# Moving the attention norm of six blocks into the stage before, through a DRAM tensor

## The chip, the cores and the metric

The kernel runs on one NeuronCore of a Trainium2 chip. It is written in Bass with the Tile layer, which places the tiles and sets the semaphores. The metric is the device time of one execution in microseconds; lower is better.

The engines are TensorE (PE, with its weight loads as PEld), VectorE (DVE), ScalarE (ACT), GpSimd (POOL) and SyncE (SP, used here to send DMAs).

## The reference

Four layers follow one another on x, 64 sequences of 64 tokens with 256 features, each with a condition vector of 64 values for each sequence:

```python
# layer 0: gated MLP with quantised activations and ternary weights
h = x * (scale * rsqrt(mean(x * x) + 1e-6))         # scale = cond @ norm_w.T + 1
val, gate = split(h @ up_w.T)
x = act_quant(val * gelu(gate)) @ weight_quant(down_w).T + x
# layer 1: attention, then SwiGLU
n = gamma * (x * rsqrt(mean(x * x) + 1e-6)) + beta  # gamma, beta from cond
x = x + alpha * attention(n)                        # 16 heads of 16 features
x = x + alpha2 * swiglu(gamma2 * rmsnorm(x) + beta2)
# layer 2: layernorm with a bias from cond; layer 3: an adapter whose weights
# are generated from cond for every sequence
```

The change concerns one term: `x * rsqrt(mean(x * x) + 1e-6)` ahead of the attention, called the attention norm here. It needs only the output of layer 0.

## The kernel before

The 4096 tokens are cut into 8 blocks of 512 tokens; a block is four tiles of 128 tokens. Three stages follow one another on the same engines. All operands of the products are float32, and a large product is made as three products of split halves (`mm3`, L87 to L89; `split` and `Splitter.turn` make the halves, the rounded one on ScalarE and the rest, by a subtraction, on VectorE or GpSimd).

**First stage** (`l0`). The loop runs over 32 tiles, n = 0 to 31, and two more steps. In step n TensorE makes the two halves of the up product (`upper(n, 0)` and `upper(n, 1)`, each with two PSUM banks); ScalarE makes the gelu (L454) and VectorE multiplies (`h`, L455). Then VectorE quantises (`quant(n)`, L461 to L466) and a DMA transposes the result (`qt`). Three steps later `lower(n - 3)` multiplies by the ternary weights (L480), and VectorE adds the input, which writes a quarter of the block's `x1` (L481). After the fourth tile of a block GpSimd sends `x1` to the DRAM tensor `x1d` (L483). In step n the output of tile n - 3 is written last, after `quant(n)`.

In between, the adapter's weights are generated: in the steps n = 5, 9, 12, 16, 19, 22, 25, 29 TensorE makes four groups of products (`gen_make`, L302, eight PSUM banks in all), ScalarE copies them out (`gen_stage`, L317), and GpSimd sends them to `s1d` and `s2d` (`gen_store`, L324). They stand between the two halves of the step. PSUM has eight banks, all shared in this stage. `hooks` is a table of more work by step: the steps 8 to 15 each split a piece of the attention weights (`splits.turn`, L221 on ScalarE and L222 on VectorE), and the steps from 25 on load and norm the first blocks of the attention and begin its products.

**Attention.** A loop over 16 units w, two to a block (`i, tp = divmod(w, 2)`). A unit computes the scores (`a_score`, L653), takes the maximum and the exponentials, transposes them on TensorE (`a_turn`, L694) with copies out of PSUM (`pts`, L696 on VectorE or L698 on ScalarE), and weighs the values of the unit before (`a_weigh`, L713, which reads `pts`). In between TensorE makes q, k and v of the next block (`a_ahead`, copied out as `qf`, `kb`, `vx`). The block after that is normed: `a_load` fetches `x1` (L588), `a_begin` squares it on ScalarE (`rms`, L236) and takes the root on GpSimd (`rsqrt`, L227 and L229), `a_scale` multiplies (`norm_tm`: L251 on ScalarE for block 2 and later, L253 on VectorE for the first two), and `norm_turn` transposes the result `xn` (L260) and applies gamma and beta (L263, L264); `split` makes `xh` and `xl` of it (L243, L244). The four PSUM banks of this stage go round in an explicit list, `pools["turn"]`, and `bank(tag, old)` says which entry from the front is taken.

**SwiGLU, layernorm and adapter** make the third stage.

The order of instructions on PE, ACT, DVE and POOL is the order in which the program issues them (`manual_schedule`). Each works strictly through its own list, so an instruction that waits holds back everything behind it. SP's DMAs are ordered by the Tile layer after the first few steps. Tiles of one tag share a fixed number of buffers: `x1` has five (`X1 = 5`, used by `xt`, `x1`, `ax1`, `ax2` and others), `xn` one, `rs`, `ss` and `st` two each. A tile that needs a buffer waits until the tile before it has been read for the last time, a store included.

Of the kernel before, what the change touches and what calls it, by code (L numbers as in the profile page):

```python
# [8 lines left out]
F32 = mybir.dt.float32  # L9
# [8 lines left out]
P = 128  # L18
NB = 64
L = 64  # L20
D = 256
# [15 lines left out]
def tile_kernel(ctx: ExitStack, tc, xT, x, condT, cw, upT, downT, qkvT, woT, ghT, outT_w,  # L37
# [6 lines left out]
    dram = ctx.enter_context(tc.tile_pool(name="dram", bufs=1, space=DRAM))  # L44
    x1d = dram.tile([NTOK, D], F32, name="x1d")
    x2d = dram.tile([NTOK, D], F32, name="x2d")
    alphad = dram.tile([3, NB, D], F32, name="alphad")
    s1d = dram.tile([2, NB, 128, BN], F32, name="s1d")
    s2d = dram.tile([2, NB, 64, D], F32, name="s2d")
# [274 lines left out]
                nc.gpsimd.dma_start(out=dst[:, :, c * GC:(c + 1) * GC], in_=stg[c * 64:(c + 1) * 64])  # L324


    def l0(hooks):
        pool = pools["a"]
        up = two(pool, "up", 2, 2 * FF)
# [141 lines left out]
        def lower(n):  # L471
            i, t = divmod(n, TT)
            am, qt = til.pop(n)
            if t == 0 and i > 0:
                blk[i][3] = block(f"x1_{i}")
            xt, x1 = blk[i][0], blk[i][3]
            nc.vector.tensor_scalar(am[:, 3:4], am[:, 1:2], wm, None, ALU.mult)
            py = bank("mm")
            for f in range(8):
                nc.tensor.matmul(py[:, :D], lhsT=qt[:, f, :], rhs=wq[:, f, :], start=f == 0, stop=f == 7)  # L480
            nc.vector.scalar_tensor_tensor(x1[:, t], py[:, :D], am[:, 3:4], xt[:, t], ALU.mult, ALU.add)  # L481
            if t == TT - 1:
                nc.gpsimd.dma_start(out=tok(x1d, i), in_=x1)  # L483
                del blk[i]

        def warm(n):

# [51 lines left out]
        for n in range(N + 2):  # L539
            if n < N:  # L540
                if n > 1:
                    upper(n, 0)
                if n == 0:
                    ternary_load()
                if n in visits:
                    for _ in range(4):
                        gen_make()
                        gen_stage()
                for _ in range(0 if n == 4 else 2 if n in visits and (n + 3 in visits or n == visits[-1]) else 1):
                    gen_load(ups[1][:, n % 2, n:n + 1] if n < 4 else None)  # L550
                    gen_store()
                upper(n, 1, "rest" if n < 2 else None)
                if n == 1:
                    ternary()
                    blk[0][3] = block("x1_0")
                if n == 4:
                    ternary_rest()
                if n % TT == 0 and n // TT + 1 < NBLK:
                    prep_load(n // TT + 1)
                if n % TT == 1 and n // TT + 1 < NBLK:  # L560
                    for _ in prep_parts(n // TT + 1):
                        pass
                if n % TT == 2 and n // TT + 1 < NBLK:
                    prep_scale(n // TT + 1)
            if n == N - 1:
                quant(n)
            for hook in hooks.get(n, ()):
                hook()

            if n < N - 1 and n != 5:  # L570
                quant(n)
            if n > 4:
                for k in range({5: 0, N + 1: N - 1}.get(n, n - 3), {N: N - 1, N + 1: N}.get(n, n - 2)):
                    lower(k)
            if n == 5:
                quant(n)


    ablk, units = {}, {}
# [6 lines left out]
    def a_load(i):  # L586
        x1 = block(f"ax1_{i}")
        nc.sync.dma_start(out=x1, in_=tok(x1d, i))  # L588
        ablk[i] = dict(x1=x1)

    def a_begin(i):
        ablk[i]["rs"] = rms(ablk[i]["x1"], f"a{i}")

    def a_scale(i):
        ablk[i]["n"] = norm_tm(ablk[i]["x1"], ablk[i]["rs"], f"a{i}", i > 1)

    def a_norm(i, c):
        norm_fm(*ablk[i]["n"], i, c, V_AG, V_AB)
# [42 lines left out]
    def a_score(w):  # L641

        i, tp = w // 2, w % 2
        pool = pools["b"]
        qf, kb = ablk[i]["qf"], ablk[i]["kb"]
        pS = banks("S", 4)
        for u in range(2):
            for m in range(2):
                for j in range(4):
                    js = slice(32 * j, 32 * (j + 1))  # L650
                    for h in range(2):
                        b = 4 * tp + 2 * u + h
                        nc.tensor.matmul(pS[h * 64:(h + 1) * 64, j, (2 * u + m) * P:(2 * u + m + 1) * P],  # L653
                                         lhsT=qf[js, m, b * L:(b + 1) * L],
                                         rhs=kb[js, m, b].rearrange("p e l -> p (e l)"),
                                         start=True, stop=True, tile_position=(32 * j, 64 * h))
        units[w] = dict(pS=pS, ex=[], pts=[], mx=pool.tile([P, 2, 32], F32, tag="mx", bufs=2, name=f"mx{w}"))

    def a_shift(w, e):

# [26 lines left out]
    def a_turn(w, e):  # L687
        U = units[w]
        pv = U["ex"][e].rearrange("p (b h) l -> p b (h l)", h=2)
        pt = pools["b"].tile([P, 2, 512], F32, tag="pts", bufs=2, name=f"pts{w}_{e}")  # L690
        for k in range(2):
            pT = bank("mm", int(e == 0 and U.get("late", False)))
            for a in range(4):
                nc.tensor.transpose(pT[:, a * P:(a + 1) * P], pv[:, 4 * k + a], ident)  # L694
            if w % 2 == 1 and k == 1:
                nc.vector.tensor_copy(pt[:, k], pT)  # L696
            else:
                nc.scalar.copy(pt[:, k], pT)  # L698
        U["pts"].append(pt)

    def a_weigh(w):
# [333 lines left out]
    hooks[last - 5] = [lambda: a_scale(0), lambda: a_load(1)]  # L1035
    hooks[last - 4] = [lambda: a_norm(0, 0), lambda: a_begin(1)]
    hooks[last - 3] = [lambda: a_norm(0, 1)]
    hooks[last - 2] = [lambda: a_scale(1), lambda: a_load(2)]
    hooks[last - 1] = [lambda: a_ahead(0, 2), lambda: a_ahead(0, 3), lambda: a_ahead(0, 4), lambda: turn_ahead(0)]
    hooks[last] = [lambda: a_ahead(0, 5), lambda: turned[0](), lambda: turn_ahead(1), lambda: a_ahead(0, 6), lambda: a_ahead(0, 7)]  # L1040
    hooks[last + 1] = [lambda: turned[1](), lambda: a_begin(2)]
    l0(hooks)
    phase.close()

# [31 lines left out]
    for w in range(W):  # L1076
# [12 lines left out]
        if tp == 1:  # L1089

            if i == 0:
                ablk[0]["at"] = load_rows(0, "alpha", 0)
            if i + 1 < NBLK:
                ablk[i + 1]["at"] = load_rows(0, ("alpha", "ab")[(i + 1) % 2], i + 1)
            if i + 3 < NBLK:
                a_load(i + 3)
            elif i + 3 == NBLK:
                f_load(0)
        a_exp(w, 0)
# [14 lines left out]
        late = []  # L1114
        if tp == 0 and i + 2 <= NBLK:
            late = [a_norm_turn(i + 2, c) for c in range(2)]
            units[w]["late"] = True
        if w > 0:
            a_project(w - 1)
        a_sum(w, 1)  # L1120
        a_recip(w)
        if 1 <= w < 14:
            splits.turn()
            if w % 4 == 0:
                splits.turn()
        if w < W - 1:
            a_turn(w, 0)
            a_turn(w, 1)
            a_rows(w)
        if tp == 1:  # L1130
            if i + 3 < NBLK:
                a_begin(i + 3)
            elif i + 3 == NBLK:
                f_begin(0)
    phase.close()
    del pools["turn"]
# [160 lines left out]
```

## Time and profile before

| | us |
|---|---|
| median of 3 runs | 748.18 (747.24 to 748.48) |
| profiled execution, whole | 749.03 |
| profiled execution, span | 746.8 |
| busy in the span: PE / PEld | 735.1 / 615.8 |
| busy in the span: DVE / ACT / POOL | 542.7 / 406.3 / 338.5 |

The profile is that of one execution. A busy time is the union of an engine's instructions. Matmuls are pipelined, so a busy TensorE is not one at its peak; a gap in it is a gap, though. In the lists by time a row gives start, duration, engine, line, operation, output<-inputs, the shapes and a count; what stands in brackets is the idle time before it and what ended that. L numbers are lines of the kernel file. In the list of waits a row gives the waiting line, what it waited for, and the total, the number and the longest of these waits. The granted clock is 1.00 where TensorE runs at full speed.

The stages are well seen in the trace: the first runs to about 259 us (the generated weights end at 230), the units of the attention from 259 to 437, and the rest to 746.8.

### The profile page before, as it was taken

Reading aid. Unit: us, or ns where it says so; the run is one execution under the profiler, and the core shown is the slowest. Engines: PE = TensorE matmul, PEld = TensorE weight load, DVE = VectorE, ACT = ScalarE, POOL = GpSimd, SP = SyncE. Lnnn points to the kernel's source line nnn. Section 1 sums busy time; section 2 is a strip of 40 time slices with the busy share of each in tenths; the row PEclk is TensorE's granted clock in tenths of the full one; section 3 lists DMA queues with packets and bytes.
Section 4 is the critical chain, followed back from the end, with each engine's and each line's share of the span. In section 5 each row is a group of like instructions: output and inputs, shape, how many; then the busy total and the mean of one; then the engine's idle time right before and its main releaser. Section 6 shows DMA issues by size and latency. Waiting matters only on the chain.

```text
span 746.8 us, 17442 instructions
## 1 busy us (share of the span) xinstructions
PE 735.1 (98%) x7036; PEld 615.8 (82%) x7036; DVE 542.7 (73%) x843; ACT 406.3 (54%) x849; POOL 338.5 (45%) x359
## 2 busy tenths in 40 slices
PE   9999999999999989999999999999999999999997
PEld 7866776777686878888898888888988888888886
DVE  4999878867687679898889886655555565655566
ACT  5553445335435579998988674535353444434242
POOL 2113233133135416766656417564646455545292
PEclk9999999999999999999999999999999999999999
DMA  7897999999965864445564247704080809080821
GB/s 252 248 266 152 290 295 213 303 276 264 307 188 111 195 155 112 120 145 153 157 156 106 54 128 184 170 25 119 23 204 12 215 2 226 1 198 2 221 62 58
DMA packets 117456, 118.87 MB, mean 159 GB/s; under 512 B 39632, under 2 KB 101200, under 8 KB 117376
## 3 DMA queue, kind: packets, MB, share of 16 engines
q1 hardware_dynamic: 109232, 91.29, 48.6%
q0 software_dynamic: 7488, 25.37, 10.8%
q8 instruction: 55, 0.90, 0.5%
q10 hardware_dynamic: 656, 1.11, 0.5%
q14 instruction: 25, 0.20, 0.1%
HBM read 71.41 MB, written 29.56 MB: 135 GB/s over the span
## 4 chain that ended last, share of the span: by engine, by line
PE 75%; DVE 14%; DMA 4%; ACT 3%; issue 2%; POOL 1%; ACTq 0%; DVEq 0%; POOLq 0%
PE gh L89 7%; PE gh L88 7%; PE gh L87 7%; PE mm L87 6%; PE mm L89 6%; PE mm L88 6%; PE acc L87 4%; PE acc L89 4%; PE acc L88 4%; PE mm L302 3%; PE mm L480 3%; PE m L87 2%; PE m L89 2%; PE m L88 2%; PE mm L964 2%
## 5 line engine op out<-in xcount | busy, mean ns | idle before, releaser
L87 PE MATMUL mm<-up,xhl 128*128 128x512 f32 x240 | 97.2, 405 | 0.0
L87 PE MATMUL gh<-xhf,gh 128*128 128x512 f32 x244 | 95.2, 390 | 0.0
L89 PE MATMUL gh<-xhf,gh 128*128 128x512 f32 x244 | 95.1, 390 | 0.0
L88 PE MATMUL gh<-xlf,gh 128*128 128x512 f32 x244 | 95.1, 390 | 0.0
L89 PE MATMUL mm<-up,xll 128*128 128x512 f32 x240 | 93.9, 391 | 0.0
L88 PE MATMUL mm<-up,xhl 128*128 128x512 f32 x240 | 93.6, 390 | 0.0
L454 ACT ACTIVATE g<-mm,rs_l 128x512 f32<-128x512 f32 x64 | 43.8, 689 | 80.8 <-PE mm L89 48.2
L804 DVE TENSOR_TENSOR sg<-gh,sg 128x512 f32<-128x512 f32 x60 | 41.2, 687 | 62.1 <-PE gh L89 32.7
L842 DVE TENSOR_TENSOR hlo<-sg,hhi 128x512 fp32r<-128x512 f32 x58 | 55.8, 963 | 34.9 <-ACT hhi L841 33.6
L841 ACT CAST hhi<-sg 128x512 fp32r<-128x512 f32 x58 | 36.0, 620 | 76.3 <-DVE sg L804 75.6
L87 PE MATMUL acc<-wout,hhi 128*128 128x256 f32 x248 | 72.0, 290 | 0.0
L89 PE MATMUL acc<-wout,hlo 128*128 128x256 f32 x248 | 69.5, 280 | 0.7 <-DVE hlo L839 0.6
L455 DVE SCALAR_TENSOR_TENSOR h<-mm,rs_l,g 128x512 f32<-128x512 f32 x64 | 46.4, 745 | 32.6 <-PE mm L89 29.6
L88 PE MATMUL acc<-wout,hhi 128*128 128x256 f32 x248 | 69.3, 280 | 0.0
L264 POOL TENSOR_TENSOR xg<-xg,cv 128x512 f32<-128x512 f32 x32 | 33.6, 1060 | 71.2 <-DVE xg L263 71.2
L87 PEld LDWEIGHTS mm<-up,xhl 128*128 128x128 f32 x240 | 45.1, 188 | 15.2 <-issue 2.4
L89 PEld LDWEIGHTS gh<-xhf,gh 128*128 128x128 f32 x244 | 45.8, 188 | 9.7
L89 PEld LDWEIGHTS mm<-up,xll 128*128 128x128 f32 x240 | 45.0, 188 | 10.1
L88 PEld LDWEIGHTS mm<-up,xhl 128*128 128x128 f32 x240 | 45.2, 188 | 8.5
L87 PEld LDWEIGHTS gh<-xhf,gh 128*128 128x128 f32 x244 | 45.8, 188 | 7.3
L88 PEld LDWEIGHTS gh<-xlf,gh 128*128 128x128 f32 x244 | 45.8, 188 | 7.3
L801 ACT ACTIVATE sg<-gh 128x512 f32<-128x512 f32 x61 | 35.9, 589 | 25.9 <-PE gh L89 25.9
(257 smaller groups left out, 1935.6 us busy)
## 6 DMA issues: line engine op xcount, KB each, us to landing
gt<-in_g SPq DMA_DIRECT2D x32, 512.0 KB, 8.1
rows<-alphad SPq DMA_DIRECT2D x48, 256.0 KB, 4.8
vb<-vx SPq DMA_DIRECT2D x32, 256.0 KB, 5.1
wd<-s1d SPq DMA_DIRECT2D x32, 256.0 KB, 6.1
wu<-s2d SPq DMA_DIRECT2D x32, 256.0 KB, 6.0
xt<-in_x SPq DMA_DIRECT2D x8, 512.0 KB, 7.4
s1d<-stgs POOLq DMA_DIRECT2D x16, 256.0 KB, 7.1
s1d<-stg POOLq DMA_DIRECT2D x16, 256.0 KB, 7.3
```

Source lines behind the costliest of these rows:

```text
L87: nc.tensor.matmul(out, lhsT=l[0], rhs=r[0], start=first, stop=False)
L88: nc.tensor.matmul(out, lhsT=l[0], rhs=r[1], start=False, stop=False)
L89: nc.tensor.matmul(out, lhsT=l[1], rhs=r[0], start=False, stop=last)
L264: nc.gpsimd.tensor_tensor(b3(xg), b3(xg), bc(vb, c, i), ALU.add)
L302: nc.tensor.matmul(pb[s][c * 64:(c + 1) * 64], lhsT=gl[h], rhs=gt[h, c * GC:(c + 1) * GC], start=True, stop=True, tile_position=(64 * s, 6 ...
L454: nc.scalar.activation(g, pg, AF.Gelu, scale=rs[:, t:t + 1])
L455: nc.vector.scalar_tensor_tensor(h[:, ch * 512:(ch + 1) * 512], pv, rs[:, t:t + 1], g, ALU.mult, ALU.mult)
L480: nc.tensor.matmul(py[:, :D], lhsT=qt[:, f, :], rhs=wq[:, f, :], start=f == 0, stop=f == 7)
L801: nc.scalar.activation(sg, pg, AF.Silu)
L804: nc.vector.tensor_tensor(sg, pv, sg, ALU.mult)
L841: nc.scalar.copy(h_hi, sg)
L842: nc.vector.tensor_tensor(h_lo, sg, h_hi.bitcast(F32), ALU.subtract)
```

## The change

For the blocks 2 to 7 (`STORED = 2`) the attention norm is made in the first stage, where `x1` is still in SBUF. `squares()` squares each tile of `x1` on ScalarE in the step after it was written, between the two halves of that step; with the fourth tile the root is taken on GpSimd. `scaled()` multiplies `x1` in place, four instructions on ScalarE, after the second half of the same step, and GpSimd sends the result to a new DRAM tensor `xnd`. Block 7's scaling is left over (`l0_rest`) and is done in unit 1 of the attention. The blocks 0 and 1 are normed as before.

In the attention `a_fetch` loads the stored result into `xn`, and `a_load` fetches `x1` itself, needed only for the residual, later (in unit 3 for block 2, one block ahead). The squares, the root and the scaling of the blocks 2 to 7 go from there. All the copies of transposed exponentials are made by ScalarE (L698); the sixteen on VectorE (L696) go. In the first unit and in the others with a `norm_turn`, the banks for the transposes are taken by a list of four numbers. The pieces of split weights (`splits.turn`) come one to each unit, behind the copies, where there were one or two ahead of them.

```diff
+    xnd = dram.tile([NTOK, D], F32, name="xnd")
...
+    STORED = 2
+    todo_sq, todo_xn, l0_rest = [], [], []
...
             nc.vector.scalar_tensor_tensor(x1[:, t], py[:, :D], am[:, 3:4], xt[:, t], ALU.mult, ALU.add)
+            if i >= STORED:
+                todo_sq.append((i, t, x1))
             if t == TT - 1:
                 nc.gpsimd.dma_start(out=tok(x1d, i), in_=x1)
                 del blk[i]
+
+        def squares():
+
+            while todo_sq:
+                i, t, x1 = todo_sq.pop(0)
+                if t == 0:
+                    til["s1"] = main.tile([P, TT], F32, tag="ss", bufs=2, name=f"s1_{i}")
+                junk = main.tile([P, D], F32, tag="junk", bufs=1, name=f"junk1_{i}_{t}")
+                nc.scalar.activation(junk, x1[:, t], AF.Square, accum_out=til["s1"][:, t:t + 1])
+                if t == TT - 1:
+                    todo_xn.append((i, x1, rsqrt(til["s1"], 1.0 / D, 1e-6, f"a{i}")))
+
+        def scaled():
+
+            if todo_xn:
+                i, x1, rs = todo_xn.pop(0)
+                for t in range(TT):
+                    nc.scalar.activation(x1[:, t], x1[:, t], AF.Copy, scale=rs[:, t:t + 1])
+                nc.gpsimd.dma_start(out=tok(xnd, i), in_=x1)
...
                 if n > 1:
                     upper(n, 0)
+                squares()
...
                 upper(n, 1, "rest" if n < 2 else None)
+                scaled()
...
+            if n >= N:
+                squares()
+                if n == N:
+                    scaled()
+        l0_rest.append(scaled)
...
-        ablk[i] = dict(x1=x1)
+        ablk.setdefault(i, {})["x1"] = x1
+
+    def a_fetch(i):
+        xn = main.tile([P, TT, D], F32, tag="xn", bufs=1, name=f"xna{i}")
+        nc.sync.dma_start(out=xn, in_=tok(xnd, i))
+        ablk.setdefault(i, {})["xn"] = xn
...
     def a_scale(i):
-        ablk[i]["n"] = norm_tm(ablk[i]["x1"], ablk[i]["rs"], f"a{i}", i > 1)
+        if i < STORED:
+            ablk[i]["n"] = norm_tm(ablk[i]["x1"], ablk[i]["rs"], f"a{i}")
+        else:
+            ablk[i]["n"] = ablk[i]["xn"], parts(f"a{i}")
...
-            pT = bank("mm", int(e == 0 and U.get("late", False)))
+            pT = bank("mm", U["old"][2 * e + k])
...
-            if w % 2 == 1 and k == 1:
-                nc.vector.tensor_copy(pt[:, k], pT)
-            else:
-                nc.scalar.copy(pt[:, k], pT)
+            nc.scalar.copy(pt[:, k], pT)
...
-    hooks[last - 2] = [lambda: a_scale(1), lambda: a_load(2)]
+    hooks[last - 2] = [lambda: a_scale(1)]
...
-    hooks[last + 1] = [lambda: turned[1](), lambda: a_begin(2)]
+    hooks[last + 1] = [lambda: turned[1](), lambda: a_fetch(2)]
...
+            if 1 <= i < NBLK - 1:
+                a_load(i + 1)
             if i + 3 < NBLK:
-                a_load(i + 3)
+                a_fetch(i + 3)
             elif i + 3 == NBLK:
                 f_load(0)
...
-            units[w]["late"] = True
+            units[w]["old"] = (1, 1, 0, 0) if w else (0, 1, 0, 0)
...
-        if 1 <= w < 14:
-            splits.turn()
-            if w % 4 == 0:
-                splits.turn()
         if w < W - 1:
             a_turn(w, 0)
             a_turn(w, 1)
             a_rows(w)
+        splits.turn()
+        if w == 1:
+            l0_rest[0]()
         if tp == 1:
-            if i + 3 < NBLK:
-                a_begin(i + 3)
-            elif i + 3 == NBLK:
+            if i + 3 == NBLK:
                 f_begin(0)
```

## The prediction

> **What bounds the kernel now.** I read the busy times by stretch first, then TensorE's own rows, then each engine in order of time around the places where TensorE stops or nearly stops, and last the waits and the landing times of the stores. In the stretches the columns are length, PE, PEld, DVE, ACT and POOL busy (instructions), granted clock, DMA share, GB/s:
>
> ```profile
> 82.00:259.00 177.00, 176.19 (x1010) 130.16 (x1016) 134.86 (x259) 82.35 (x184) 54.62 (x80) 1.00 0.90 242
> 268.00:272.00 4.00, 3.52 (x31) 3.35 (x39) 0.88 (x2) 2.26 (x5) 0.80 (x1) 0.57 1.11 212
> 273.00:437.00 164.00, 161.78 (x2735) 143.79 (x2735) 146.91 (x164) 142.57 (x290) 96.39 (x91) 1.00 0.47 123
> ```
>
> TensorE fills the first stage from 82 us on (0.8 us idle in 177) and the attention (2.2 idle in 164). Work taken off another engine is therefore worth only what TensorE waits for it, and a late result on another engine costs as soon as TensorE runs out of free PSUM banks. In the attention these are the waits (total, times, longest):
>
> ```profile
> PEld m L713 <- DVE pts L696: 3.1, 7, 0.4
> PE m L713 <- DVE pts L696: 2.0, 7, 0.3
> ```
>
> At the seam between the stages, in order of time:
>
> ```profile
> 263.56 1.69 ACT L251 ACTIVATE xna<-ax,rs_a 128x256 f32<-128x256 f32 x4
> 268.49 3.38 PE L694 MATMUL m<-ident,ex 128*128 128x128 f32 x16 [2.00 <-ACT kb L635]
> ```
>
> In the first stage, around the 16th iteration (n=16), whose generation of weights (L302) TensorE begins at 125.75:
>
> ```profile
> 117.06 0.39 ACT L221 CAST wo<-st 128x256 fp32r<-128x256 f32 x1
> 121.36 0.40 ACT L221 CAST wo<-st 128x256 fp32r<-128x256 f32 x1
> 122.55 0.81 POOL L483 DMA_DIRECT2D x1d<-x  x1 [3.99 <-DVE x L481]
> 123.49 0.42 DVE L222 TENSOR_TENSOR wo<-st,wo 128x256 fp32r<-128x256 f32 x1
> 127.15 0.48 DVE L481 SCALAR_TENSOR_TENSOR x<-mm,am,xt 128x256 f32<-128x256 f32 x1
> 127.55 0.74 DVE L455 SCALAR_TENSOR_TENSOR h<-mm,rs_l,g 128x512 f32<-128x512 f32 x1
> ```
>
> VectorE has no gap from 110 to 128 and runs some 5 us behind TensorE. And at n=29, with the landing times of x1d's loads and stores together:
>
> ```profile
> 228.06 1.94 PE L302 MATMUL mm<-gt,gl 64*64 64x512 f32 x14 [0.81 <-DVE x L481]
> DMA to landing us min/median/max: 3.9/5.8/9.0
> ```
>
> There VectorE was the late one and TensorE already paid 0.81.
>
> **The change part by part: the attention.** Six blocks lose 4 squares (L236, start to start 0.54, 2.1 us a block) and 4 scalings (L251, 1.7) on ScalarE, 22.8 us; it gains 16 copies of about 0.54 (L698), 8.6; VectorE loses 16 copies (L696), 9.8 us. None of that is a bound by itself. What counts:
>
> (a) Odd units. VectorE's two copies (348.83 to 350.05 in one unit) end after TensorE reached L713 at 349.28. All four now go to ScalarE, which comes free of the two xha casts at 347.34 (the gh cast moves behind them) and ends them at about 349.4: nearly the whole wait goes, and a rest of some 0.1 us stays. Bounds 0 and 3.1; I take 2.5 gained, nearer to the PEld row.
>
> (b) Unit 0. Without L251 the ScalarE chain to kb ends about 1.2 us earlier, and the transposes start in a bank freed by vx instead of kb: 0.45 us of them before that wait. Wait 2.00 plus slow transposes (3.38 against 1.91 in later units) is 3.5 to be had. Against that, the squares of block 7 now stand ahead of the last xha cast (256.78), and the fetch of xn must land before the transposes at 264.2: issued after the last transposes of block 1 (253.5) plus 6.1 for a load, it has 4 us; issued where the fourth ax load stood (261.93) it lands at 268, 4 us late. Bounds 3.5 gained and 4 lost; I take 2.5 gained.
>
> Reloads cost nothing elsewhere: a fetch goes out some 15 us before its transposes (340.4 against 355.7) and takes 6.1; without that cover it would cost the 6.1. The moved split turns keep their number, 16, and stand behind the copies: nothing.
>
> **The first stage.** ScalarE is busy 82 of 177 us, so 13 us of squares and 8.5 of scalings fit by volume. The order is what costs. A square of tile n-4 stands between the two gelus of iteration n and waits for VectorE's L481 of the iteration before; the gelu, the weight-generation copies (L317) or a cast behind it wait too. And the scaling overwrites x1, so it must wait until the store of the same x1 to x1d, sent one iteration earlier, has landed. Its store to xnd waits in turn on POOL for the scaling; POOL's s1d and s2d stores queue behind that.
>
> The dearest place, n=14 to 16. Tile 10 is written at 116.86; square 0.54, so the second gelu goes from 114.45 to 117.40; it takes 0.6, the four squares behind it 2.0, the cast 0.4: 120.4, where L222 stood at 118.09, so VectorE slips 2.3. Tile 11 is then written at 124.55 and its block's store sent at 124.85; it landed 4.4 after issue, so 129.25; four scalings (1.69) 130.9; cast 131.3. The L222 of 123.49 slips by 7.8, and with it L481, from 127.63 to 135.4. TensorE's eight generation banks need this bank in the last quarter, 125.75 + 24/32 of 3.59 = 128.4: stall 7.0. Without the first slip the same sum gives 4.7; if a bank is found elsewhere or ScalarE catches up, 0. I take 7.0, since VectorE has no gap there.
>
> Tile 8 at n=12: written 99.58, square 0.54, first copy 0.53, 100.65 against the end of the generation at 99.98: 0.7. n=19: 151.07 + 1.1 = 152.15 against 152.34: 0.3 for the following product. n=22: 175.25 + 1.1 = 176.3 against 175.31: 1.0. Bounds for the three together 0 and 3.
>
> n=23 to 25: the store of block 4, sent at 183.35, landed after 9.0, at 192.35; scaling to 194.0; first gelu of n=24 (187.06) at 194.0, square, second gelu to 195.8, h 4.6 late, h(25) done at 201.0 against a need at 197.4: 3.6. With the 4.4 of the other store it is hidden. I take 2.0.
>
> n=27 to 29: five x1 buffers are all in use (xt6, xt7, x1 of block 5, ax0, ax1); x1 of block 6 gets the buffer of block 5, now free only when xnd has landed. Its store to x1d, 216.12 plus 4.0, is at 220.1; scaling 221.8; second store 4.4 more, 226.2. L481 of tile 24 (220.92) slips by 5.3, and the wait that ended at 228.06 by as much. Bounds 0 and 5.3 (a buffer that the allocator finds free otherwise); I take 4.0.
>
> (c) Clock. After the 2.00 us gap the clock was 0.57 for four us and 16 transposes took 1.5 us more; two of these stalls are longer. Bounds 0 and 3; I take 2.0. The Trainium skill (TensorE: Matmul & The Clock Gate, "Why this matters for your kernels") asks only that PE-idle gaps stay under about 3 us; this trace shows the fall after 2.0. By the page the stalls of n=25 would carry no clock cost, which does not move the sum.
>
> The Trainium skill (DMA: Bandwidth & Descriptors, "Anatomy of one DMA") says a DMA's semaphore fires only when the last byte is confirmed landed, slowest towards HBM, and gives 2.0 us plus bytes at 436 GB/s, an estimate of 3.2 us for these 512 KB; the trace has 4.0 to 9.0. It speaks against overwriting a tile whose store is on its way; by its figure n=16 would lose 1.2 us less.
>
> Sum: 7.0 + 0.7 + 0.3 + 1.0 + 2.0 + 4.0 + 2.0 = 17.0 lost, 2.5 + 2.5 = 5.0 gained, net 12.0 slower. The profiled execution took 749.03 (span 746.8), so 761.0; it lies 0.85 above the median of the runs, 748.18, so 760.2 there.
>
> **The rivals.** Hidden first stage, so faster: every late ScalarE result is caught up before TensorE lacks a bank. For it: ScalarE is idle over half the time, and the 4.66 us that it waited for xg ahead of n=29 cost only 0.81. It decides if VectorE's slips stay below about 1 us at the generating iterations. Then 5.0 is gained, or 5.6 with (a) and (b) somewhat higher: 743 (741 to 746). Against: a cast that VectorE waits for stands behind the scaling at n=15.
>
> Half of it: one of the two large stalls happens (7.0 or 4.0) and the small ones fall into slack: 4 to 7 less 5, between -1 and +4 with a little clock: 750 (747 to 752).
>
> Worse: the six extra stores run in a stretch with a DMA share of 0.90, all stores land after 9.0 as block 4's did, and every scaling blocks as long: three blocks more at some 3 us, 770.
>
> That the change does not do what it says has no place: rows L236 and L251 for six blocks must leave the attention.
>
> **How the numbers follow.** My forecast, slower by several of these stalls (752 to 768), 0.60; hidden and faster 0.20; half 0.15; worse 0.05. Range 743 to 768: it leaves out part of the faster case and the worse one. Runs of this kernel tell 0.2% (1.5 us) from no change; the half case gives 0.05 to the same and 0.10 to slower. Faster 0.20, same 0.05, slower 0.75.
>
> **What would show it.** Right: in the first stage ScalarE's L251-like scaling waits for DMA x1d, TensorE's L302 waits for DVE x or h near n=16 and n=29, a clock below 1.00 there, and the stage ends 12 to 18 us later; odd units without a wait on DVE pts; unit 0's transposes in under 2.5 us. Wrong: if the first stage ends within 2 us of 259, the scalings cost nothing and the time falls to 743; if unit 0 waits for DMA xnd, (b) has turned round.

## The result and the profile after

The changed kernel takes 768.76 us (median of 4 runs, 764.16 to 771.86) against 748.05 for the kernel before beside it: ratio 1.0273 [1.0218, 1.0328], 20.7 us slower. The forecast was 760.2 with a range to 768: the direction holds, the size does not, and the time lies 0.8 above the range. The profiled execution of after took 769.91, its span is 768.1, 21.3 more than before. Times and ratios here and below are of fast runs; one slow run of the last kernel, 762.9, is left out.

First the stretches of after, read as those of before (length, PE, PEld, DVE, ACT, POOL busy, granted clock, DMA share, GB/s):

```profile
82.00:259.00 177.00, 161.35 (x834) 109.42 (x833) 116.03 (x220) 82.72 (x210) 51.76 (x80) 0.94 0.83 228
...
273.00:437.00 164.00, 162.82 (x2714) 145.14 (x2712) 138.85 (x159) 137.22 (x264) 94.10 (x88) 1.00 0.67 174
```

From 82 to 259 us TensorE was busy 176.19 of 177 before; now 161.35, and at a clock of 0.94. ScalarE's busy time there is 82.72 against 82.35: the added squares and scalings are in it, but the stage is slower and less of the old work got into the stretch. So it is not the volume of ScalarE's work that limits the stage; the rows below show that it is the order.

Around n=16, where the forecast put its dearest place, in order of time (ScalarE, VectorE, TensorE):

```profile
126.09 0.42 ACT L499 ACTIVATE junk<-x 128x256 f32<-128x256 f32 x1 [3.71 <-DVE x L485]
...
130.19 1.70 ACT L508 ACTIVATE x<-x,rs_a 128x256 f32<-128x256 f32 x4 [3.02 <-DMA x1d<-x]
131.80 0.39 ACT L222 CAST wo<-st 128x256 fp32r<-128x256 f32 x1
132.10 0.68 ACT L458 ACTIVATE g<-mm,rs_l 128x512 f32<-128x512 f32 x1
```

```profile
121.83 0.42 DVE L223 TENSOR_TENSOR wo<-st,wo 128x256 fp32r<-128x256 f32 x1 [1.57 <-ACT wo L222]
...
132.22 0.42 DVE L223 TENSOR_TENSOR wo<-st,wo 128x256 fp32r<-128x256 f32 x1 [4.26 <-ACT wo L222]
...
135.90 0.48 DVE L485 SCALAR_TENSOR_TENSOR x<-mm,am,xt 128x256 f32<-128x256 f32 x1
```

```profile
127.12 2.79 PE L303 MATMUL mm<-gt,gl 64*64 64x512 f32 x18
132.83 1.98 PE L303 MATMUL mm<-gt,gl 64*64 64x512 f32 x6 [2.92 <-ACT g L458]
136.44 2.63 PE L303 MATMUL mm<-gt,gl 64*64 64x512 f32 x8 [1.63 <-DVE x L485]
139.00 0.79 PE L88 MATMUL mm<-up,xhl 128*128 128x512 f32 x1
139.59 0.63 PE L89 MATMUL mm<-up,xhl 128*128 128x512 f32 x1
140.02 0.63 PE L90 MATMUL mm<-up,xll 128*128 128x512 f32 x1
```

This is the forecast chain link by link: the scaling (L508) waits for the store of the x1 that it overwrites, the cast (L222) stands behind it, VectorE's L223 idles 4.26 for the cast, L485 comes at 135.90 and with it a PSUM bank. The forecast had the end of the cast at 131.3 and that of L485 at 135.4; they are at 132.2 and 136.4, in a trace that was 1.4 late before this place. One link is new: the longer of TensorE's two gaps, 2.92, ends with the gelu (L458 at 132.10) that stands behind the cast in ScalarE's list; the forecast had only the wait for L485.

Now look at TensorE behind the gaps. The 32 generating matmuls run from 127.12 to 139.00, 11.88 us against 3.59 in the trace of before, and only 2.92 + 1.63 of that is idle. Products that start 0.23 apart at full clock start 0.43 apart from 139.59 on.

At n=27 to 29 (VectorE's row, then TensorE's) the third chain of the forecast is there too: the buffer for x1 is held until the store to xnd has landed.

```profile
247.63 0.48 DVE L485 SCALAR_TENSOR_TENSOR x<-mm,am,xt 128x256 f32<-128x256 f32 x1 [6.11 <-DMA xnd<-x]
```

```profile
248.16 4.49 PE L303 MATMUL mm<-gt,gl 64*64 64x512 f32 x18 [3.94 <-DVE x L485]
...
255.35 3.45 PE L303 MATMUL mm<-gt,gl 64*64 64x512 f32 x14 [2.69 <-DVE x L485]
```

The granted clock tells why. From 82 us to the end of the stage it is below 1.00 in four stretches, at the three long stalls (same columns as above):

```profile
132.76:143.00 10.24, 8.54 (x23) 4.02 (x24) 4.05 (x8) 5.09 (x12) 4.98 (x9) 0.50 1.07 334
214.68:218.09 3.41, 3.39 (x10) 1.31 (x11) 0.62 (x1) 3.35 (x9) 1.59 (x3) 0.50 0.94 254
248.81:252.22 3.41, 3.41 (x17) 1.25 (x16) 2.85 (x6) 0.87 (x2) 1.04 (x1) 0.50 0.00 0
255.64:259.05 3.41, 3.41 (x15) 0.83 (x8) 0.31 (x1) 3.39 (x9) 2.07 (x5) 0.50 0.64 121
```

Together they are 20.47 us at half clock, 10.2 us of full clock lost. The waits of the whole run that name the squares and the scaling (total, times, longest), with the landing times of x1d's loads and stores together:

```profile
ACT junk L499 <- DVE x L485: 54.2, 20, 5.6
ACT x L508 <- DMA x1d<-x: 19.2, 4, 7.9
```

```profile
DMA to landing us min/median/max: 3.2/5.1/8.7
```

At the seam and in the units the forecast gains appear. The transposes of unit 0 wait 0.52 where they waited 2.00 for kb, and in the waits of the attention what is left ahead of the weighing is ScalarE's:

```profile
295.66 1.61 PE L734 MATMUL m<-ident,ex 128*128 128x128 f32 x12 [0.52 <-DVE xg L264]
```

```profile
PEld m L750 <- ACT pts L735: 1.2, 7, 0.2
```

To say where the time went, I compare the start of the same instruction in both traces: the products of `lower` in each step and the first scores of each unit. The delay against before grows only in the generating steps, and shrinks in the attention:

| up to | forecast | delay added | of it new idle of TensorE |
|---|---|---|---|
| n=12 | 0.7 | 1.4 | 0.5 |
| n=14 to 16 | 7.0 | 10.1 | 4.5 |
| n=19 | 0.3 | 1.2 | 0.3 |
| n=22 | 1.0 | 1.7 | 0.9 |
| n=23 to 25 | 2.0 | 5.0 | 2.7 |
| n=27 to 29 | 4.0 | 9.6 | 5.8 |
| clock | 2.0 | 10.2 (in the rows above) | |
| first scores of unit 0 | 17.0 lost | 28.9 lost | 14.8 |
| unit 0 | 2.5 gained | 3.5 gained | |
| units 1 to 15 | 2.5 gained | 4.2 gained | |

The idle at n=29 is 3.94 + 2.69 less the 0.81 that stood there before. From the last unit on nothing more happens (0.1): 28.9 - 3.5 - 4.2 + 0.1 = 21.3.

### The profile page after: what moved, and what is told of

The parts are those of the page before. It is cut to its first block, busy times and chain, and to the rows that moved or that the text cites. A ratio compares the mean times of both kernels' runs of the same rounds, so it can differ in the third digit from the quotient of the medians.

```text
span 768.1 us, 17507 instructions
## 1 busy us (share of the span) xinstructions
PE 744.6 (97%) x7036; PEld 617.0 (80%) x7036; DVE 534.3 (70%) x827; ACT 411.3 (54%) x865; POOL 343.5 (45%) x365
## 3 DMA queue, kind: packets, MB, share of 16 engines
q10 hardware_dynamic: 656, 1.11, 0.5%
## 4 chain that ended last, share of the span: by engine, by line
PE 60%; DVE 6%; DMA 4%; ACT 4%; issue 2%; POOL 1%; SPq 0%; DVEq 0%; ACTq 0%; POOLq 0%
PE gh L90 7%; PE gh L89 7%; PE gh L88 7%; PE acc L88 4%; PE acc L89 4%; PE acc L90 4%; PE m L90 3%; PE m L88 3%; PE m L89 3%; PE m L734 3%; DMA xt<-in_x 2%; PE S L693 2%; PE m L750 2%; PE mm L1001 2%; DMA x1d<-x 2%
## 5 line engine op out<-in xcount | busy, mean ns | idle before, releaser
L88 PE MATMUL mm<-up,xhl 128*128 128x512 f32 x240 | 98.5, 410 | 0.1
L89 PE MATMUL mm<-up,xhl 128*128 128x512 f32 x240 | 94.4, 393 | 0.0
L458 ACT ACTIVATE g<-mm,rs_l 128x512 f32<-128x512 f32 x64 | 43.6, 686 | 38.3 <-PE mm L90 17.0
L303 PE MATMUL mm<-gt,gl 64*64 64x512 f32 x256 | 42.5, 695 | 15.9 <-DVE x L485 12.9
```

The lines of the kernel that those rows point to most:

```text
L88: nc.tensor.matmul(out, lhsT=l[0], rhs=r[0], start=first, stop=False)
L89: nc.tensor.matmul(out, lhsT=l[0], rhs=r[1], start=False, stop=False)
L303: nc.tensor.matmul(pb[s][c * 64:(c + 1) * 64], lhsT=gl[h], rhs=gt[h, c * GC:(c + 1) * GC], start=True, stop=True, tile_position=(64 * s, 6 ...
L458: nc.scalar.activation(g, pg, AF.Gelu, scale=rs[:, t:t + 1])
```

## The experiments

**The parts alone.** Three kernels split the change into its attention part, the squares and the scaling. The first two leave out the norm of the six blocks, the third leaves out its root, so they serve for their times only.

```diff
 # attention alone
-            if i >= STORED:
-                todo_sq.append((i, t, x1))
-        nc.sync.dma_start(out=xn, in_=tok(xnd, i))
+        nc.sync.dma_start(out=xn, in_=tok(x1d, i))
 # squares alone: squares and roots as in the change; these lines go, fetch from x1d
-                for t in range(TT):
-                    nc.scalar.activation(x1[:, t], x1[:, t], AF.Copy, scale=rs[:, t:t + 1])
-                nc.gpsimd.dma_start(out=tok(xnd, i), in_=x1)
 # scaling alone: no squares, a constant in place of the root
-                    todo_xn.append((i, x1, rsqrt(til["s1"], 1.0 / D, 1e-6, f"a{i}")))
+                    todo_xn.append((i, x1, nhalf))
```

> Leaves out the squares, the roots, the scaling and the store to xnd in the first stage; the attention fetches x1 unscaled from x1d in place of xnd, so the norm of six blocks is missing. Everything of the change in the attention stays. Theory (three waits in the first stage cost 29 us and the attention gains 7.6): the first stage is as before, S of unit 0 near 258.8, and the time is 748.05 - 7.6 = 740.4. Rival (the attention gains only its own old waits, 2.5 + 2.5, and the rest of the 7.6 was only lateness of the first stage that the seam absorbed): 743.

> Leaves out the scaling and the store to xnd; squares and roots stay where the change has them; the attention fetches x1 unscaled from x1d. Theory (the squares cost by standing ahead of the second gelu, of the copies and of the casts while they wait for L481): about 1.5 at n=12, 2 at n=16, 1 at n=19, 1.6 at n=22, 1 at n=29, together 7 above the kernel with the attention part alone: 747. Rival (it is the volume of ScalarE's work and the squares, 13 of 21.5 us of it, cost 60% of the 29): 757.

> Leaves out the squares and roots; the scaling in place and the store to xnd stay, with a constant (-0.5) in the place of the root. Theory (the scaling waits for the landing of x1d, block 6's x1 waits for the landing of xnd, each with a slow clock after it): 6 at n=16, 3 at n=25, 8 at n=29, together 17 above the attention part alone: 757, with ScalarE waiting for DMA x1d and DVE L485 for DMA xnd. Rival (volume: 8.5 of 21.5 us, 40% of 29): 752, and no such wait before TensorE's gaps.

Measured: attention alone 741.64 (0.9912 [0.9896, 0.9928]), squares alone 754.73 (1.0082 [1.0063, 1.01]), scaling alone 753.99 (1.0082 [1.0056, 1.0109]). The attention part is worth 6.6 us, between its two expectations. Squares cost 13.1 over it, far more than the theory's 7 and nearer to its rival; scalings cost 12.35, between the two expectations. 741.6 + 13.1 + 12.35 = 767.1, 1.7 short of the whole. That the totals add up is luck, since the places don't: at n=16 squares alone add 3.0 and scaling alone 1.9, together they add 10.1. The difference is about what the clock lost there, 5.1: in the two kernels alone the granted clock is 1.00 around n=16 (126 to 146 and 124 to 145 us), in the change it is 0.50 for 10.24 us. At n=25 squares alone cost nothing, at n=29 they cost 3.7, which the forecast had not seen at all.

**The order of the squares, and the wait for the store.** In the first kernel the squares stand behind the second gelu instead of between the gelus. In the second the scaling writes a tile of its own and so need not wait for the store of x1. The third does both.

```diff
                 if n > 1:
                     upper(n, 0)
-                squares()
...
                 upper(n, 1, "rest" if n < 2 else None)
+                squares()
                 scaled()
```

```diff
-            qt = pool.tile([P, 8, P], BF16, tag="qt", bufs=5, name=f"qt{n}")
+            qt = pool.tile([P, 8, P], BF16, tag="qt", bufs=4, name=f"qt{n}")
...
+                xo = pools["a"].tile([P, TT, D], F32, tag="xo", bufs=1, name=f"xo{i}") if i < 7 else x1
                 for t in range(TT):
-                    nc.scalar.activation(x1[:, t], x1[:, t], AF.Copy, scale=rs[:, t:t + 1])
-                nc.gpsimd.dma_start(out=tok(xnd, i), in_=x1)
+                    nc.scalar.activation(xo[:, t], x1[:, t], AF.Copy, scale=rs[:, t:t + 1])
+                nc.gpsimd.dma_start(out=tok(xnd, i), in_=xo)
```

> The whole change with squares() moved behind the second half of the step, so that nothing of that half waits for L485; the scaling stays in place behind it. Theory: the losses at n=12, 19 and 22 (4.3 together) go and 3 to 4 of the 10 at n=16 and 2 of the 9.6 at n=29: 758 to 761. Rival (the store waits alone make the stalls, the place of the squares is nothing): 767 to 769.

> The whole change, but the scaling of blocks 2 to 6 writes into a tile of its own instead of over x1 (block 7 stays as it was; one of five qt buffers gives the room). Theory (two separate causes: squares in the way of the second gelu, 13.1 us by the run with squares alone; and scalings that wait for the store of the same x1, 12.35 by the run with scalings alone): the scaling no longer waits for a store and keeps only its own 1.7 us a block, and the x1 buffers are free as early as before; 741.6 + 13.1 + about 2 = 757 (754 to 760), with no wait of ACT on DMA x1d except for block 7. Rival (what costs is the extra work in ScalarE's order and the extra six stores, not the wait): 765 to 769. A second rival, that the missing qt buffer itself costs, would show as waits for qt and would end above 760 as well.

> As the kernel with its own scaling tile, and the squares behind the second half of the up projection instead of between the halves. Theory: squares that late cost what the run with late squares left over the run with scalings alone, 756.7 - 754.0 = 2.7, and the scaling about 2 as its waits are gone: 741.6 + 2.7 + 2 = 746 (743 to 750), so a little faster than before. Rival (the six extra stores, or the missing qt buffer, cost by themselves): 752 to 758. By either, the part after the first stage is as in the whole change, 7.6 us shorter than before.

Measured: late squares 756.71 (1.0122 [1.0086, 1.0157]), 12.0 less than the whole change and 1.3 below the range that I had expected; own tile 758.71 (1.0142 [1.0126, 1.0157]), 10 less, as the theory had it; both 749.59 (1.0026 [1.0012, 1.004]), 19.2 less. The two causes are thus separate, and between them they are most of the loss. Squares that stand late cost 2.7 over scaling alone (756.71 and 753.99) where early ones cost 14.8 over the same kernel (768.76): their place costs, not their volume. TensorE has no wait for qt from 82 to 290 us in the own tile's trace, so the fifth qt buffer, which made room for the tile, is not seen to cost. But the third kernel, though inside its range, is 3.6 above the 746 that I had expected, and the own tile's profile says why. Its ScalarE and GpSimd at n=15, in order of time:

```profile
128.72 1.70 ACT L509 ACTIVATE xo<-x,rs_a 128x256 f32<-128x256 f32 x4 [1.99 <-POOL rs_a L230]
130.33 0.39 ACT L222 CAST wo<-st 128x256 fp32r<-128x256 f32 x1
```

```profile
125.84 0.81 POOL L489 DMA_DIRECT2D x1d<-x  x1 [3.14 <-DVE x L485]
126.74 0.19 POOL L228 TENSOR_SCALAR ms_a<-s 128x4 f32<-128x4 f32 x1
127.66 1.03 POOL L230 TENSOR_TENSOR rs_a<-ms_a,nhalf 128x4 f32<-128x4 f32 x1 [0.74 <-DVE h L459]
```

The store's landing is no longer waited for, and the scaling starts only 1.47 earlier (128.72 against 130.19), 0.45 of which is that this run was that much ahead: GpSimd's root was the next late thing behind the store. So at n=16 the own tile wins almost nothing (the delay added there is 9.0 against 10.1); it wins at n=25, where nothing is added now, and at n=29 (4.7 against 9.6). With both edits GpSimd's root is what the scaling waits for, in all waits of the first stage:

```profile
ACT xo L509 <- POOL rs_a L230: 17.1, 5, 5.5
```

**The price of a gap by itself.** The kernel before, with VectorE held up twice by operations that nobody reads. The expectation counts by tile: tiles 12 and 20 are written in the steps 15 and 23.

```diff
+            for _ in range({12: 40, 20: 25}.get(n, 0)):
+                nc.vector.tensor_scalar(idle, idle, 1.0, None, ALU.mult)
             nc.vector.scalar_tensor_tensor(x1[:, t], py[:, :D], am[:, 3:4], xt[:, t], ALU.mult, ALU.add)
```

> The kernel before, with VectorE held twice in the first stage: ahead of the products' result at n=12 by 40, and at n=20 by 25, operations of 128x128 on a tile that nobody reads (about 0.2 us each, an estimate from the 0.42 of 128x256: some 8 and 5 us). It measures a TensorE gap's price by itself. Theory (clock): TensorE loses more at each place than the gap that its rows show, by 2 to 5 us, since its matmuls run at about half clock after it; with gaps of about 4 to 6 and 2 to 3 the loss is 10 to 14 together, 758 to 762, and the granted clock of the 10 us behind the gaps is 0.7 to 0.85. Rival (a gap costs its own length, and the rest of the change's loss came from elsewhere): the loss equals the gaps, 754 to 757, clock 0.95 or more.

Measured: 755.32 (1.0094 [1.0079, 1.0108]), 7.4 more than before. VectorE's hold first, then TensorE:

```profile
126.85 10.96 DVE L482 TENSOR_SCALAR idle<-idle 128x128 f32<-128x128 f32 x40
```

```profile
148.51 1.09 PE L302 MATMUL mm<-gt,gl 64*64 64x512 f32 x8
151.08 3.24 PE L302 MATMUL mm<-gt,gl 64*64 64x512 f32 x18 [1.49 <-DVE x L483]
156.27 1.08 PE L302 MATMUL mm<-gt,gl 64*64 64x512 f32 x6 [1.94 <-DVE x L483]
157.28 0.76 PE L87 MATMUL mm<-up,xhl 128*128 128x512 f32 x1
157.84 0.63 PE L88 MATMUL mm<-up,xhl 128*128 128x512 f32 x1
...
160.80 0.40 PE L89 MATMUL mm<-up,xll 128*128 128x512 f32 x1
161.04 0.39 PE L87 MATMUL mm<-up,xhl 128*128 128x512 f32 x1
```

```profile
148.51:157.35 8.84, 5.42 (x34) 1.53 (x33) 7.88 (x16) 4.77 (x13) 2.40 (x4) 1.00 0.26 57
157.35:160.76 3.41, 3.41 (x8) 2.72 (x9) 0.00 (x0) 1.62 (x3) 3.41 (x6) 0.50 1.02 237
```

The total lies in the rival's range; of the mechanism the theory has half. The hold of 10.96 us cost nothing for 22 us, then TensorE lost 6.7 at n=19; the second hold cost 0.8 at n=25. At n=19 the rows show 1.49 + 1.94 = 3.43 idle. The rest is slow work: the 32 generating matmuls take 8.77 from start to end against 3.59 warm, so 5.18 more, 1.75 beyond the gaps; and the next 24 products take 6.26 against 4.71. 3.43 + 1.75 + 1.55 = 6.73. Only the 1.55 is the clock's: it is 1.00 until 157.35, behind the last generating matmul, and then 0.50 for 3.41 us, which is worth 1.7. The 1.75 was lost at full clock, by generating matmuls that start in ones and threes where they start in fours in the trace of before. I read that as their banks coming free one by one; no run separates it. What I got wrong in the total was the gaps: VectorE's slack took most of the hold.

The same sum for the whole change at n=16: 11.88 - 3.59 = 8.29 for the generating matmuls, 4.55 of it idle; 6.52 - 4.72 = 1.80 for the next 24 products; 10.09 together, the delay of the table. So 5.5 is slow work, 5.1 of it the clock's. At n=25 it gives 2.71 idle and 2.2 slow (clock 1.7), at n=29 5.8 idle and 3.4 slow (clock 3.4).

**Which part of the attention gains.** Attention alone, with the sixteen copies back on VectorE:

```diff
-            nc.scalar.copy(pt[:, k], pT)
+            if w % 2 == 1 and k == 1:
+                nc.vector.tensor_copy(pt[:, k], pT)
+            else:
+                nc.scalar.copy(pt[:, k], pT)
```

> The attention part alone (no squares, roots or scaling of the six blocks anywhere, x1 fetched in place of xn), with the odd units' copies of the second half of each pair back on VectorE as in the kernel before. It splits the 6.6 us that the attention part gained alone. Theory (the gain after unit 0 is the wait of PE on VectorE's copies): odd units lose 0.3 to 0.6 each again, 741.6 + 4 = 745.6 (744.5 to 746.5), and waits of PE on DVE pts are back. Rival (the gain comes from the squares and scalings that left ScalarE): within 1 us of 741.6.

Measured: 742.45 (0.992 [0.9907, 0.9933]), 0.8 above attention alone, inside the rival's bound. TensorE's waits for VectorE's copies are all back (the two rows below name the same stalls, once by the products and once by the weight loads), and cost 0.8, or 1.8 by the spans of the profiled executions (741.2 and 739.4).

```profile
PE m L751 <- DVE pts L734: 2.0, 7, 0.3
PEld m L751 <- DVE pts L734: 3.1, 7, 0.4
```

**Mended versions.** Four kernels look for one that keeps the 6.6 us. The first keeps only squares (late ones) and roots in the first stage, and loads x1 and scales it on VectorE in the attention. The second is the third kernel of the order's group, with roots that have a place of their own, and with the scaling behind the step's casts. The third also leaves the squares out of generating steps. The fourth puts the root ahead of the store to x1d and of that step's stores to s1d and s2d in GpSimd's list (the cut shows the first of these).

```diff
 # roots only
-                for t in range(TT):
-                    nc.scalar.activation(x1[:, t], x1[:, t], AF.Copy, scale=rs[:, t:t + 1])
-                nc.gpsimd.dma_start(out=tok(xnd, i), in_=x1)
-            ablk[i]["n"] = ablk[i]["xn"], parts(f"a{i}")
+            ablk[i]["n"] = norm_tm(ablk[i]["x1"], kept[:, i], f"a{i}")
 # scaled later
-                    todo_xn.append((i, x1, rsqrt(til["s1"], 1.0 / D, 1e-6, f"a{i}")))
+                    nc.gpsimd.tensor_scalar(til["s1"], til["s1"], 1.0 / D, 1e-6, ALU.mult, ALU.add)
+                    nc.gpsimd.tensor_tensor(kept[:, i], til["s1"], nhalf, ALU.pow)
+                    todo_xn.append((i, x1, kept[:, i]))
-                scaled()
...
             for hook in hooks.get(n, ()):
                 hook()
+            if n < N:
+                scaled()
 # no squares in generating steps
-                squares()
+                if n not in visits:
+                    squares()
 # root first: as scaled later, and behind the root
+                    if i < 7:
+                        nc.gpsimd.dma_start(out=tok(x1d, i), in_=x1)
```

> Squares and roots of six blocks in the first stage, behind the second half of the up projection, the eight roots kept; nothing is scaled or stored there. In the attention x1 is loaded as before and scaled by VectorE; all four transposed copies on ScalarE as in the change. Theory: 741.6 for the attention without norm, 2.7 for the late squares, and four scalings a block of about 0.42 on VectorE, 6 x 1.7 = 10 us, that lost 9.8 us of copies there, so hidden but for about 1: 744 to 746, faster than both kernels. Rival (VectorE's scalings stand ahead of the softmax work of a unit and TensorE waits for them in six units, as it did for its copies): 6 x 1.7 more, 751 to 755.

> The change with its scaling in a tile of its own and late squares, where the scaling still waited 17 us in all for GpSimd's roots with a cast and gelus behind it; here the roots have a place of their own and the scaling stands behind the iteration's casts, ahead of the next products. Theory (what is left of the loss, 6.8 us, is ScalarE's order at n=15 and n=27): n=16 loses under 1.5 instead of 4.9 and n=29 under 2 instead of 3.1, 745 (743 to 747), faster than before. Rival (the stall only moves, to the gelus and copies of the generating iterations): 748 to 751.

> As the kernel with the later scaling, and no squares in the eight iterations that generate weights: they follow one iteration later. Theory (generating iterations are the only ones in which a slip costs): up to 1 us less than that kernel, 744 (742 to 747). Rival (squares two tiles at a time make the roots and the scaling late, and x1's buffers with them): 2 to 6 us more than that kernel.

> As the kernel with the later scaling, but on GpSimd's queue the root stands ahead of the x1d store of the same block and of that iteration's s1d or s2d stores (they follow it). In the kernel with the later scaling, the scaling at n=15 still waited 3.12 us for GpSimd's root, which stood behind 2.0 us of DMA issues. Theory (the root's place in GpSimd's queue is what is late next, once the store's landing is out of the way): the scaling at n=15 starts some 2 us earlier, n=16 loses under 1.5 where it lost 3.0, and the time is 745 to 747. Rival (the generating iterations lose anyway, to the copies and the second gelu behind the scaling, or x1d stored later holds x1's buffers): 748 to 750.

Measured: roots only 749.67 (1.0021 [1.0007, 1.0035]), scaled later 748.37 (0.9996 [0.9979, 1.0012]), no squares in generating steps 748.14 (1.0007 [0.9986, 1.0027]), root first 753.59 (1.0061 [1.0036, 1.0087]). None beats the kernel before.

Roots only missed the 744 to 746 expected of it, though not by the rival's stall. The first stage loses 3.8 by the first scores, unit 0 gives back 2.6, and from unit 1 to unit 15 the gain is 0.1, where attention alone has 4.7. VectorE's scalings probably take the units' gain away: TensorE waits for them by name in its trace, but for 1.0 us in all, and the rest I can't place.

Scaled later adds 2.7 at n=16 and 1.8 at n=29 by its trace, less than the 4.8 and 3.1 of the kernel that it mends, but more than the 1.5 that I had expected at n=16. It brings the change to the time of before and no further, which is the rival's range. Much of what it saves is clock: it has no stretch below 1.00 in the first stage, where the kernel that it mends has one of 3.41 us at 0.50 at each of the two places. At n=29 the idle time is the same in both (the kernel with both edits first, then scaled later; the gap, then the clock from 228 to 242 us):

```profile
233.54 3.28 PE L303 MATMUL mm<-gt,gl 64*64 64x512 f32 x14 [2.42 <-DVE x L485]
228.00:242.00 14.00, 11.58 (x63) 6.05 (x62) 8.01 (x13) 8.30 (x21) 7.51 (x10) 0.88 0.62 166
```

```profile
232.89 1.94 PE L303 MATMUL mm<-gt,gl 64*64 64x512 f32 x14 [2.41 <-DVE x L486]
228.00:242.00 14.00, 11.59 (x70) 7.18 (x63) 9.22 (x16) 9.32 (x23) 8.26 (x10) 1.00 0.57 152
```

Leaving the squares out of the generating steps changed nothing that the runs can tell (748.14 and 748.37).

Root first did what it was built for: the scaling at n=15 starts at 125.85 after 1.11 of waiting, in place of 128.52 after 3.12, and the delay behind n=16 is 0.85 in all, in place of 3.0. And it is the slowest of the four, outside both expectations. Its profiled execution took 758.08, more than most of its runs. TensorE waits there at other places as well, here three from one profile, with the landing times of qt from 82 to 256 us behind them:

```profile
147.09 1.05 PE L485 MATMUL mm<-wq,qt 128*128 128x256 bf16 x8 [1.17 <-DMA qt<-q]
...
210.75 1.05 PE L485 MATMUL mm<-wq,qt 128*128 128x256 bf16 x8 [1.61 <-DMA qt<-q]
...
241.30 2.74 PE L303 MATMUL mm<-gt,gl 64*64 64x512 f32 x14 [3.61 <-DVE x L486]
```

```profile
DMA to landing us min/median/max: 3.1/8.2/22.1
```

In the kernel before these landings are 3.0/5.6/11.6. The DMA share from 82 to 256 us is 1.01 here and 0.90 in the kernels scaled later and before. The stores bunched behind the root are a candidate, but not a sufficient one: the kernel with late squares, whose stores stand where the change has them, waited longer for qt, with landings as late (same window; the wait counted from 82 to 290 us):

```profile
PE mm L484 <- DMA qt<-q: 5.8, 2, 3.1
```

```profile
DMA to landing us min/median/max: 3.0/6.7/22.0
```

I did not vary the stores by themselves, and why root first is slower stays open.

## Why the prediction was right and wrong

- **Direction and chains: right.** The three chains of the forecast (the square ahead of the gelu, the scaling behind its block's store, the x1 buffer held by the second store) are rows of the trace after, the one at n=16 within 1 us of the forecast times. Taking the squares out of the gelus' way or the stores out of the scaling's way gives back 12.0 and 10 us, both together 19.2.
- **The idle: right in sum, in part by luck.** The six stall terms sum to 15.0; TensorE's new idle is 14.8. Single places are off, and the errors cancel: 4.5 instead of 7.0 at n=16, 5.8 instead of 4.0 at n=29, and squares cost at n=29 as well.
- **The step that failed: (c), the clock,** 2.0 with bounds 0 and 3. Measured, it is 10.2 us: 20.47 us at a granted clock of 0.50. I took one gap's row as the price for the whole change. In the trace of before that row is one stretch of 3.41 us at 0.50, worth 1.7; the trace of after has six times that length, one stretch each behind the gaps of 2.71, 3.94 and 2.69 us and three in a row at n=16, where two gaps fall into one group. It is not one execution's bad luck: the mean granted clock of the four runs is 0.984 to 0.990, which by the same sum is 7.6 to 12.3 us.
- **A second loss had no term:** 28.9 - 14.8 - 10.2 = 3.9 us are neither idle rows nor clock. Some 2.5 of them lie at n=12, 19 and 22, where the clock is 1.00 and the generating matmuls start further apart, as in the kernel with two holds; 1.4 I can't place.
- **What would have been right:** with (c) as measured, 15.0 + 10.2 - 5.0 = 20.2 slower, 768.4. That this comes so close is luck again: the 3.9 of slow work that is missing in it and 2.7 of gain that is missing too largely cancel. The trace of before had the price of one stretch, 1.7; one for each of the three long stalls would have made 5.1, still half of what came. That n=16 would bring three was not to be read from it.
- **The gain (b), unit 0: right** in kind, 3.5 at the upper bound instead of 2.5. The fetch of xn came in time.
- **The gain (a): too small, and wrong in cause.** The units gain 4.2, above the bound of 3.1, but the wait for VectorE's copies, which was to give 2.5, is worth only 0.8 to 1.8. With the copies back on VectorE the units still gain 3.0. Whether this remainder comes from squares and scalings that left ScalarE, or from the new order of banks and split turns, was not separated.
- **The rivals.** Hidden, and half of it, fall by the first stage's clock and idle. The worse case names nearly the measured time, 770, but by stores that all land after 9.0 and a scaling that blocks at each; the landings have a median of 5.1, four of six scalings waited, and most of the extra time is the clock's.

The Trainium skill (TensorE: Matmul & The Clock Gate, "Why this matters for your kernels") asks for no idle gaps over about 3 us; here 1.49 and 1.94 us in one group (two holds), 2.06 us (own tile and late squares) and 2.71 us (the change) were each followed by a clock of 0.50, so the measurement decides against that threshold. The kept traces give no sharp one in its place. From 82 us on, every gap of 2.8 us or more in the first stage came with such a stretch; of the shorter ones some were (1.69 us in roots only), some not (2.15 in squares alone, 2.29 in scaling alone, 2.41 in scaled later). The same page ("A second HAM failure mode: psum-queue depth-cycling") says that short, frequent idling between groups of matmuls, as PSUM banks come round, makes the clock swing and costs throughput between bursts. The two gaps in one group at n=16, with a clock of 0.50 for 10.24 us, come nearest to that; five gaps of 1.6 to 3.9 us in 177 us are not frequent idling, so this trace does not test it.

## What to carry to other kernels

Price a stall of a full TensorE place by place, by its idle time and by 1.7 us more for every 3.41 us at half clock that may follow, and carry that second part as a range: here it was nothing after some gaps of 2.4 us, one such stretch after others, and three after two gaps in one group. Before moving work to an engine with idle time, look at what is queued behind it at the places where the bound engine needs its last buffer; a scaling in place behind a store puts a DMA's landing into that queue. And when one late thing is taken away, name the next (here the store, then GpSimd's root, then late landings of qt) before counting the gain.

## What the hardware showed beyond that

- The granted clock fell from 1.00 to 0.50 in the first stage for 3.41 us, or for three times that, 10.24 us (the change and own tile, each time at n=16 behind two gaps in one group), never for another length. Two kernels with the same gap at n=29, 2.42 and 2.41 us, differ in it: one has the fall, the other not.
- VectorE, held for 10.96 us, cost nothing in the step where it was held and 6.7 us in the next generating step, 22 us after the hold began: a stall's row can lie far from its cause.
- The root of 128x4 values takes GpSimd 1.0 to 1.5 us, more than the square of a whole 128x256 tile on ScalarE (0.42).
- The transposing transfers landed after 8.2 us in the median and 22.1 at most in root first, and after 6.7 and 22.0 in late squares, where the kernel before has 5.6 and 11.6; what delays them was not found.
